# Three attention branches summed in 32-row blocks turned by VectorE, a band mask in sixteen 32x32 tiles, and a new order of instructions

## The chip, the cores and the metric

The kernel runs on one core of a Trainium2 chip. A core has TensorE (PE, matmuls into PSUM), VectorE (DVE), ScalarE (ACT) and GpSimd (POOL), and SyncE (SP), which issues the transfers. The metric is the device time of the whole program in microseconds: the median of three runs before the change was 1501.98 us (1499.52 to 1504.33).

## The reference

The input `x` has 8 batch rows of 512 tokens and 256 features. After a layer norm, three results are added to `x`: an attention with three branches, a gated feed-forward layer of 1024 features, and a mixture of 1024 rank-one experts of which 8 are chosen for each of 4 expert heads. All matrices are float32. The attention has 16 heads of 16 features, and its part that matters here is, per head and token:

```python
# compressed: 16 tokens of k and of v make one block (32 blocks)
logits_c = where(pos >= blk_end, q @ k_c.T / 4, NEG)
out_c = softmax(logits_c) @ v_c * any(pos >= blk_end)
# selected: the tokens of the 4 blocks with the highest logits_c
out_s = softmax(where(tok <= pos, q @ k_s.T / 4, NEG)) @ v_s
# local: the last 32 tokens
out_l = softmax(where(0 <= pos_q - pos_k <= 32, q @ k.T / 4, NEG)) @ v
gates = softmax(mean over heads of q @ Wg + bg)          # three per token
out = (gates[0] * out_c + gates[1] * out_s + gates[2] * out_l) @ Wo
```

No softmax is normalised before its product with `v`: each `v` carries a column of ones, so a product gives 16 sums and their denominator, 17 columns per head. The sums are divided, weighted with the gate and added at the end. This is the "branch sum" of the title.

## The kernel before, in words

The work is cut into 32 tiles of 128 tokens (four per batch row, `i` = 0 to 3) and 16 halves of 256 tokens for the feed-forward layer. For each tile, row or half there are generator functions, one for each stage, and each says which engine and which buffers its next piece needs. A `Conductor` (L209) runs all of them at build time: it books each instruction on its engine with a price (`price`, L233: so much per column and a fixed part, 0.36 us for an issue by SyncE) and takes next the stage that can start first, ties broken by a rank. `PLAN` (L116) shifts the ranks, tile by tile. What comes out is one fixed order of instructions per engine, with semaphores where they depend on each other. At run time an engine takes its queue strictly in that order, so an instruction that waits holds all that stands behind it. Every instruction is emitted by one helper, so the profile names L202 for all of them; I go by the tiles (`acs`, `at`, `wT` and so on).

Eight PSUM banks are shared by all: two pairs for the attention logits, four single banks for everything else. The stages around the change are:

- `gates` (L657): the three gates per token of a row, `gt`, tokens on partitions.
- `queries` (L767): `q` of a tile, and the compressed logits for all 32 blocks of the row, masked by a matmul with the identity that adds `cmask`.
- `select` (L855): picks the four blocks on VectorE; GpSimd subtracts each head's maximum from the compressed logits into `ec`.
- `compressed` (L955): ScalarE exponentiates `ec`, TensorE transposes it (`ecT`), and four matmuls with the block-diagonal `vc17` give the compressed sums, tokens on partitions. VectorE divides them by the 17th column and multiplies by the gate into `atc`.
- `weights` (L987): logits of the local and the selected branch, keys on partitions, 32-row tiles of TensorE, four at a time. The local ones get the band mask by four matmuls of 128x128 by 512 columns with the identity and `bandT`. ScalarE exponentiates into `wT`.
- `products` (L1046): `wT` times `v17`, with four heads in the four 32-row groups of the output: 17 of the 32 rows are sums. Two banks hold selected and local branch for all heads, tokens along the columns.
- `finish` (L1081) with `by_token` (L938): for each of the two banks ScalarE copies it to `acs`, TensorE transposes it (4 transposes) into another bank, so that tokens are on partitions; VectorE divides and weights the two branches into `at2`; GpSimd adds them and `atc`; TensorE transposes the sum (`at`), and ScalarE copies it to `attnT`, features on partitions.
- `project` (L1311): adds the expert part and `attnT` times `wo`, and stores the tile.
- `route` (L1194): four chains of GpSimd products (`big`) per tile, which build the weights of all 1024 experts from VectorE's `chosen`. `hidden` (L1269) with `fetch` (L1261): the feed-forward layer, whose weights `wb` are loaded again by SyncE for each half into two buffers.

Of the kernel before, what the change touches and what calls it, by code (L numbers as in the profile page):

```python
# [16 lines left out]
P = 128  # L17
# [25 lines left out]
    ("ident", P), ("any", 1), ("slot", 8), ("fold", 2 * P), ("head4", H), ("last", 2),  # L43
]
_BF_COLS = [
    ("identb", P), ("win", P + WIN), ("caus", P), ("causT", P), ("bandT", P), ("prevT", WIN),
# [17 lines left out]
def shape_constants():  # L64
# [21 lines left out]
    put("head4", p // NB == np.arange(H)[None] % 4)  # L86
# [6 lines left out]
    putb("bandT", np.where((q - p >= 0) & (q - p <= WIN), 0.0, OUT))  # L93
# [14 lines left out]
def bc(ap, axis, n):  # L108
# [8 lines left out]
    "-10",  # L117
    "-12",
    "-5 -5 2 -1 -3 -11 0 -1",
    "-30 5 0 -14 0 -5 12 -4",  # L120
    "0 7 6 -4 0 0 10 4",
    "-7 5 4 0 9 25 -10 6",
    "-1 3 -1 23 3 14 4 -30 -30 -2 -7 -11 -2 -20 4 3 -9 -6 30 1 3 -1 3 4 2 14 -7 2 6 -8 10 23",
    "-3 0 2 -4 8 0 0 -4 -2 0 -4 -1 -7 -4 1 0 3 2 0 -7 0 2 0 1 -21 -2 0 -3 23 -9 7 -10",
    "-1 0 24 30 12 4 10 0 29 4 -1 -30 5 3 1 0 20 26 6 30 0 9 1 13 18 -1 13 16 -10 16 28 21",
    "4 0 -5 0 0 3 3 -27 0 -5 -6 -30 -15 -28 2 -16 8 6 -13 9 -29 -25 0 -13 -17 12 3 -6 0 -14 28 "
    "2",
    "-1 7 7 0 11 -14 18 -30 0 -12 1 -12 -2 19 0 -7 8 0 0 0 7 0 6 -24 -24 -28 13 -19 10 -23 -21 "
    "7",
    "-19 -18 12 -8 0 -17 -3 -20 -19 3 1 0 -4 -14 -1 -12 -1 -26 9 2 7 5 -1 -2 3 -14 -9 -12 0 0 "  # L130
    "8 -11",
    "0 -4 -25 -23 4 -7 -17 -30 -30 -2 -1 -29 -13 -30 -2 -11 -24 0 -4 -27 -28 -30 9 -3 -9 -2 "
    "-27 0 0 -9 2 16",
    "0 -7 -21 -2 -1 -5 -7 -6 0 -30 0 -25 -3 -3 10 -3 7 0 17 15 6 12 0 0 0 2 22 5 29 -28 30 0",
    "-6 0 0 16 5 10 -8 5 17 -14 1 8 -26 -9 0 0 4 0 2 4 -10 -7 1 -3 14 -27 26 -3 15 2 -10 13",
    "-3 1 0 0 3 0 -3 -4 1 2 2 -30 0 -10 3 1 3 -5 0 -4 10 2 0 7 11 0 6 0 0 -2 14 28",
    "-14 9 -8 -1 -10 -3 1 27 -13 0 3 1 -7 1 -4 6 -12 -24 -2 1 3 -18 -6 7 21 1 -2 9 -13 0 4 15",
    "-2 -29 0 -7 3 -1 -30 0 0 -18 -3 0 11 0 11 -10 -12 0 -7 30 -27 -24 0 -3 -13 -1 16 8 1 -10 "
    "24 23",
    "-1 0 -10 0 0 -30 -7 18 -3 2 11 1 -11 11 -20 7 -7 4 0 7 8 -3 12 -5 0 4 -25 8 -25 0 -14 12",  # L140
    "20 1 0 -3 7 6 18 7 -18 4 -8 1 -14 -6 1 -8",
    "0 7 0 -7 0 -3 7 1 0 4 0 0 -2 -3 8 15",
    "-16 19 19 6 -10 6 -8 15 1 0 -5 1 7 6 12 21 -20 15 26 3 -4 -7 -1 -8 -9 -5 6 9 -9 -15 -25 0",
    "-28 10 -28 13 -3 0 4 -11 0 12 19 -21 -5 -14 28 -26 -2 0 26 17 13 -29 25 -23 17 0 0 26 -2 "
    "7 12 0",
# [60 lines left out]
class Conductor:  # L206
# [26 lines left out]
    def price(self, eng, op, args, kw):  # L233
# [3 lines left out]
        if eng == "PE":  # L237
            self.tiling = (P, P)
            if op == "transpose":
                cost = 0.109  # L240
            else:
                n = int(np.prod(args[2].shape[1:]))
                cost = n * 0.433e-3 if args[2].dtype == BF16 else max(n * 1.69e-3, 0.223)
                if self.share > 1:
                    k, m = args[1].shape[0], int(np.prod(args[1].shape[1:]))
                    self.tiling = tuple(32 if a <= 32 else 64 if a <= 64 else P for a in (k, m))
                    each = 1.05 if m > 32 else 0.97 if n > 64 else 1.25
                    cost = max(n * 0.423e-3 * each, 0.017)
        elif eng == "SP":
            cost = 0.36  # L250
        else:
# [4 lines left out]
            if eng == "POOL" and any(a.dtype == BF16 for a in aps):  # L256
                cost += 0.24e-3 * n
            if op in ("match_replace", "max_index", "tensor_tensor_reduce", "reciprocal"):
                cost += 0.08
# [69 lines left out]
def tile_kernel(ctx, tc, x, wq, wk, wqT, wv, wo, bdk, bdv, wga, bga, wgu, bg, bu, wd, bd,  # L329
# [64 lines left out]
    ident, identb = const("ident"), bconst("identb")  # L394
    cmask = bconst("cmask").rearrange("p (i n) -> p i n", n=NB)
# [37 lines left out]
    vc17s = stock("vc17_", 2, [P, H * D1])  # L433
    for st_, fill in ((v17s, 1.0), (vl17s, 0.0), (vc17s, 0.0)):
# [7 lines left out]
    for it in vc17s.items:  # L442
        pool.tensor_copy(by_head(it[0])[:, :, D], const("head4"))
# [23 lines left out]
    gts = stock("gt", 3, [P, 3, NT])  # L467
# [8 lines left out]
    ecTs, acss = stock("ecT", 1, [P, 4, P]), stock("acs", 2, [P, 4, P])  # L476
    rzs = stock("rzn", 3, [P, 16])
    atcs, at2s = stock("atc", 2, [P, 16, D]), stock("at2", 2, [P, 2, 2, 4 * D])
# [20 lines left out]
    for e in con.at:  # L499
        con.at[e] = 0.0  # L500

# [155 lines left out]
    def gates(s, pg):  # L657

        s.gt = yield DVE, gts
        gt, gm = s.gt.ap, buf_gm  # L660
# [13 lines left out]
        vec.tensor_tensor(gt[:, 2, 0:1], gt[:, 2, 0:1], const("any"), ALU.mult)  # L674
        s.done("gates")
# [3 lines left out]
    def prepare_values(s):  # L679
# [53 lines left out]
        s.vc17 = yield None, vc17s  # L733
        vc17 = s.vc17.ap
        pt = yield PE, banks
        pvt = pt.ap[:, :2 * P].rearrange("p (c n) -> p c n", c=2)
        for f in range(2):
# [4 lines left out]
        vec.tensor_tensor(by_head(vc17)[:, :, :D], pvt.rearrange("p c (h d) -> p (c h) d", d=D),  # L742
                          bc(const("head4"), 2, D), ALU.mult)
# [7 lines left out]
    def release_row(s):  # L751
# [8 lines left out]
        for it in (s.vc17, s.v17, s.vl17):  # L760
            it.free()
        yield None, s.tiles[-1].ev("at0"), s.tiles[-1].ev("at1")
        s.gt.free()
# [3 lines left out]
    def queries(t):  # L767

        s, i = t.row, t.i
        yield None, s.ev("xn"), came["wq_s"]  # L770
# [13 lines left out]
        pt, t.lg = yield PE, banks, lgs  # L784
        for a in range(2):
            mm(pt.ap[:, a * 8 * NB:(a + 1) * 8 * NB], t.q.ap[:, a, :],
               s.kcbd.ap[:, a].rearrange("p h n -> p (h n)"), start=a == 0, stop=False,
               skip_group_check=True)
        pc = pt.ap.rearrange("p (h n) -> p h n", n=NB)
        first = i * (P // G)  # L790
        mm(pc[:, :, first:], identb, bc(cmask[:, i, first:], 1, H), start=False, stop=True,
           skip_group_check=True)
        yield ACT,
        act.copy(t.lg.ap[:, :, 4:], pc)
# [60 lines left out]
    def select(t):  # L855
# [13 lines left out]
        pool.tensor_tensor(t.ec.ap, lg[:, :, 4:], bc(mx, 2, NB), ALU.subtract)  # L869
# [68 lines left out]
    def by_token(acs, dst, gates):  # L938

        pt = yield PE, banks  # L940
        p4 = pt.ap.rearrange("p (a g d) -> p a g d", a=4, g=4)
        for a in range(4):
            pe.transpose(p4[:, a].rearrange("p g d -> p (g d)"), acs.ap[:, a, :], ident)
        acs.free()
        rzn = yield DVE, rzs
        po = p4.rearrange("p a g d -> p (a g) d")
        vec.reciprocal(rzn.ap, po[:, :, D])
        for b in range(2):
            c = slice(8 * b, 8 * b + 8)
            vec.scalar_tensor_tensor(dst[:, c], po[:, c, :D], gates[:, b:b + 1],  # L950
                                     bc(rzn.ap[:, c], 2, D), ALU.mult, ALU.mult)
        pt.free()
        rzn.free()

    def compressed(t):  # L955

        s, i = t.row, t.i
        yield ACT, t.ev("ec")
        act.activation(t.ec.ap, t.ec.ap, AF.Exp)
        pt, ecT = yield PE, banks, ecTs  # L960
        for g in range(4):
            pe.transpose(heads4(pt.ap)[:, g, :],
                         t.ec.ap[:, 4 * g:4 * g + 4, :].rearrange("p h n -> p (h n)"), ident)
# [4 lines left out]
        yield None, s.ev("vc"), s.ev("gates")  # L968

        pt = yield PE, banks  # L970
        w = 4 * D1
        for g in range(4):
# [445 lines left out]
```

## Time and profile before

| what | value |
|---|---|
| median of three runs | 1501.98 us |
| the profiled execution | 1506.37 us in all, span of its instructions 1504.3 us |
| TensorE granted clock, mean | 0.989 |
| idle of TensorE, 0 to 35 us / 35 to 200 / 200 to 1470 / 1470 to 1505 | 16.5 / 11.7 / 32.2 / 3.9 us |
| longest waits of GpSimd | 164.6 us for VectorE's `chosen` |
| longest waits of ScalarE | for TensorE's PSUM: 160.4 (`xg`), 140.5 (`wT`), 123.8 us (`aT`) |
| DMA | 83.5 MB, mean 56 GB/s |

The page gives for each engine its busy time, its share of the span and its count of instructions. A group's line has the engine, the operation, what it writes and reads, the shape, the count, then the busy time in us, the mean of one in ns, and the engine's idle time just before them with what ended it. The timeline has start and length in us. TensorE's matmuls are pipelined, so their lengths overlap, and the distance between two starts tells more than a length. A float32 matmul leaves two records, a transpose and a bf16 matmul one.

### The profile page before, as it was taken

The numbers are of one execution on the slowest core, as the hardware profiler recorded it, in microseconds if no ns is written. First come the engines' busy times: TensorE is split into PE (matmuls) and PEld (weight loads), VectorE is DVE, ScalarE is ACT, GpSimd is POOL, SyncE is SP. The second block draws the span as 40 slices with busy tenths as digits, with TensorE's granted clock in tenths as the row PEclk, the third lists the DMA queues.
The fourth block names the chain that finished last, engine by engine and source line by source line (L and its number), as shares of the span: only waits on it lengthen the run. The fifth ranks groups of instructions, "written<-read, shape, count | busy, mean of one in ns | idle before, by whom it ended". The sixth has DMA issues, their size and how long they took to land.

```text
span 1504.3 us, 44379 instructions
## 1 busy us (share of the span) xinstructions
PE 1440.8 (96%) x17312; PEld 1126.9 (75%) x17312; DVE 1300.7 (86%) x5207; ACT 649.0 (43%) x1292; POOL 962.5 (64%) x948
## 2 busy tenths in 40 slices
PE   5899998999999999999999999999999999999999
PEld 4677777777777777777877778777877777877777
DVE  3989889979989988899889896989798978999992
ACT  3534451544354445452544425444434435344253
POOL 3546756755567566874675756777636775577676
PEclk9899999999999999999999999999999999999999
DMA  8111111212112112121122212022120112111120
GB/s 287 44 45 50 36 53 32 80 46 60 47 31 79 45 43 58 51 62 51 30 61 62 60 47 62 25 67 59 48 66 26 55 48 60 52 27 52 37 59 19
DMA packets 100018, 83.52 MB, mean 56 GB/s; under 512 B 23265, under 2 KB 80609, under 8 KB 99681
## 3 DMA queue, kind: packets, MB, share of 16 engines
q1 hardware_dynamic: 99808, 80.69, 18.4%
q8 instruction: 136, 2.23, 0.6%
q14 instruction: 74, 0.60, 0.1%
HBM read 49.67 MB, written 4.19 MB: 36 GB/s over the span
## 4 chain that ended last, share of the span: by engine, by line
PE 66%; DVE 24%; ACT 3%; issue 2%; POOL 2%; DMA 2%; SPq 0%; DVEq 0%; ACTq 0%; POOLq 0%
PE psum L202 66%; DVE bm L202 3%; DVE pick L202 2%; DVE big L202 1%; POOL big L202 1%; DVE sums L202 1%; DVE chosen L202 1%; DVE ml L202 1%; DVE at_x L202 1%; DVE aT L202 1%; ACT wT L202 1%; DVE hT L202 1%; DVE xg L202 1%; DVE mr L202 1%; DVE at L202 1%
## 5 line engine op out<-in xcount | busy, mean ns | idle before, releaser
L202 POOL TENSOR_TENSOR big<-chosen,ed 128x1024 f32<-128x1024 bf16 x128 | 275.1, 2149 | 250.1 <-DVE chosen L202 164.6
L202 ACT ACTIVATE wT<-psum 128x1024 f32<-128x1024 f32 (+1 forms) x224 | 218.4, 1024 | 149.6 <-PE psum L202 140.5
L202 PE MATMUL psum<-xnT,wb 128*128 128x256 f32 x1024 | 250.4, 388 | 9.2 <-DVE hT L202 6.9
L202 POOL TENSOR_TENSOR big<-big,ed 128x1024 f32<-128x1024 f32 x128 | 248.6, 1942 | 9.9
L202 PEld LDWEIGHTS psum<-xnT,wb 128*128 128x128 f32 x1024 | 187.4, 191 | 45.4 <-DVE hT L202 9.2
L202 DVE TENSOR_REDUCE bm<-psum 128x32 f32<-128x512 f32 (+2 forms) x224 | 199.5, 912 | 18.6 <-PE psum L202 18.2
L202 POOL TENSOR_TENSOR big<-big 128x512 f32<-128x512 f32 x128 | 141.0, 1102 | 9.6
L202 PE MATMUL psum<-wT,v 128*32 128x128 f32 (+1 forms) x3584 | 127.6, 278 | 7.4 <-ACT wT L202 5.3
L202 ACT ACTIVATE xg<-psum,bg_s 128x256 f32<-128x256 f32 x128 | 60.9, 476 | 162.0 <-PE psum L202 160.4
L202 PEld LDWEIGHTS psum<-xnT,deT_s 128*128 128x128 f32 x1024 | 122.1, 193 | 10.5 <-issue 4.9
L202 PE MATMUL psum<-xnT,deT_s 128*128 128x128 f32 x1024 | 127.0, 277 | 0.0
L202 PE MATMUL psum<-wd_s,hT 128*128 128x256 f32 x512 | 124.7, 387 | 1.2 <-DVE hT L202 0.8
L202 PE MATMUL psum<-ue_s,aT 128*128 128x256 f32 x512 | 121.8, 384 | 0.2 <-DVE aT L202 0.2
L202 PEld LDWEIGHTS psum<-wT,v 128*32 128x32 f32 (+1 forms) x3584 | 90.5, 110 | 40.3 <-ACT wT L202 16.5
L202 DVE SCALAR_TENSOR_TENSOR aT<-aT,psum 128x512 f32<-128x512 f32 x128 | 86.6, 680 | 27.3 <-ACT aT L202 23.5
L202 PEld LDWEIGHTS psum<-ue_s,aT 128*128 128x128 f32 x512 | 94.0, 190 | 21.3 <-issue 5.4
L202 PEld LDWEIGHTS psum<-wd_s,hT 128*128 128x128 f32 x512 | 94.0, 192 | 20.6 <-issue 4.2
L202 PE MATMUL psum<-k,q 32*128 32x384 f32 (+3 forms) x1024 | 98.0, 474 | 5.8 <-DMA k<-kT 5.7
L202 DVE TENSOR_TENSOR chosen<-rc 128x1024 bf16<-128x1024 bf16 x128 | 99.4, 776 | 0.0
L202 POOL TENSOR_TENSOR gw<-big 128x256 f32<-128x256 f32 x128 | 90.6, 707 | 10.0
L202 PE MATMUL psum<-qx,k 32*128 32x128 f32 (+1 forms) x2560 | 94.3, 282 | 1.8 <-ACT wT L202 1.3
L202 PEld LDWEIGHTS psum<-qx,k 32*128 32x128 f32 (+1 forms) x2560 | 78.4, 182 | 21.9 <-issue 14.6
(158 smaller groups left out, 2911.3 us busy)
## 6 DMA issues: line engine op xcount, KB each, us to landing
wb<-in_wgu SPq DMA_DIRECT2D x128, 256.0 KB, 2.7
qx<-qT SPq DMA_DIRECT2D x96, 64.0 KB, 1.9
qx<-xT SPq DMA_DIRECT2D x96, 64.0 KB, 1.9
yo<-in_x SPq DMA_DIRECT2D x32, 128.0 KB, 2.1
q<-qT SPq DMA_DIRECT2D x64, 64.0 KB, 2.0
k<-kT SPq DMA_DIRECT2D x16, 256.0 KB, 2.5
out<-yo SPq DMA_DIRECT2D x32, 128.0 KB, 1.7
kw<-k SPq DMA_DIRECT2D x48, 80.0 KB, 2.5
```

The lines of the kernel that those rows point to most:

```text
L202: return f(*a, **k)
```

## The change

Five things change together.

1. Compressed logits are computed and masked for the `nb` = 8 (i + 1) blocks that can be seen, not for all 32; `ec` is laid out with the four head groups inside.
2. The compressed product is turned round: `vcq` is the stationary operand and `ecT` moves, so its sums come out like those of `products`, 32 rows per head group, tokens along the columns. `products` writes the columns in four runs of 32 tokens.
3. `acs`, `by_token`, `at2`, `atc` and the last transpose go. VectorE turns the three banks out of PSUM by 32x32 blocks into `accT` (one buffer), so that tokens are on 32 partitions, by block and head. A new stage `join` divides (48 denominators per partition in one reciprocal), multiplies by the gates on VectorE, weights and adds on GpSimd, and turns the sum back by 32x32 blocks into `attnT`.
4. For that the gates are needed by token in a block and for each head group: SyncE copies them with 16 small transfers per row from `gt` to `gx`.
5. The band mask becomes 16 matmuls of 32x32 by 512 columns, each in its own tile of TensorE (four row groups by four column groups), with a table `bandR` in place of `bandT`.

The planner's prices get two additions (the sixteen tiles, GpSimd's memset), SyncE's queue is booked as busy until 21 us at the start, and `PLAN` has new numbers throughout, so the order of instructions differs on every engine. In the order that results, SyncE issues the spreads of the first `k` and `q` directly behind the constants, where two `wb` chunks and four `yo` loads stood first.

```diff
-        for a in range(2):
-            mm(pt.ap[:, a * 8 * NB:(a + 1) * 8 * NB], t.q.ap[:, a, :],
-               s.kcbd.ap[:, a].rearrange("p h n -> p (h n)"), start=a == 0, stop=False,
-               skip_group_check=True)
+        pc = pt.ap[:, :H * nb].rearrange("p (h n) -> p h n", n=nb)
+        for a in range(2):
+            mm(pc[:, 8 * a:8 * a + 8], t.q.ap[:, a, :], s.kcbd.ap[:, a, :, :nb], start=a == 0,
+               stop=False, skip_group_check=True)
...
-        mm(pc[:, :, first:], identb, bc(cmask[:, i, first:], 1, H), start=False, stop=True,
+        mm(pc[:, :, first:], identb, bc(cmask[:, i, first:nb], 1, H), start=False, stop=True,
...
+        s.gx = yield SP, gxs
+        for c in range(4):
+            for g in range(4):
+                sp.dma_start(out=s.gx.ap[32 * g:32 * g + 32, c], in_=gth.ap[32 * c:32 * c + 32])
...
-        for g in range(4):
-            mm(pt.ap[:, g * w:g * w + w], ecT.ap[:, g, :], s.vc17.ap[:, g * w:g * w + w],
-               start=g == 0, stop=g == 3, skip_group_check=True)
+        pc = pt.ap.rearrange("p (b j q) -> p b j q", b=4, j=4)
+        for j in range(4):
+            mm(pc[:, :, j, :], s.vcq.ap[:, j, :], ecT.ap[:, j, :].rearrange("p (b q) -> p b q", b=4),
+               start=j == 0, stop=j == 3, skip_group_check=True)
...
-        rzn = yield DVE, rzs
-        po = by_head(pt.ap[:, :H * D1])
-        vec.reciprocal(rzn.ap, po[:, :, D])
-        vec.scalar_tensor_tensor(t.atc.ap, po[:, :, :D], s.gt.ap[:, 2, i:i + 1], bc(rzn.ap, 2, D),
-                                 ALU.mult, ALU.mult)
+        t.accT = yield DVE, accTs
+        vec.transpose(t.accT.ap[:, 2].rearrange("p b j m -> p (b j m)"), pt.ap)
         pt.free()
...
+            if k is None:
+                con.share = 16
+                for c in range(4):
+                    for j in range(4):
+                        r = slice(32 * j, 32 * j + 32)
+                        mm(heads4(es[j // 2].ap[32 * c:32 * c + 32, j % 2]), identb[r, r],
+                           bc(bandR[r, c], 1, 4), start=False, stop=True, skip_group_check=True,
+                           tile_position=(32 * j, 32 * c))
+                con.share = 1
...
-            acs, at2h = yield ACT, acss, at2s
-            act.copy(acs.ap, heads4(t.acc[jp].ap))
-            t.acc[jp].free()
-            at2 = at2h.ap
-            yield from by_token(acs, at2.rearrange("p b j (g d) -> p (b j g) d", d=D),
-                                s.gt.ap[:, 0:2, i])
...
-            pt = yield PE, banks
-            pe.transpose(pt.ap[:, :P], at, ident)
-            at2h.free()
-            yield ACT,
-            act.copy(t.attnT.ap[:, jp, :], pt.ap[:, :P])
+            yield DVE, t.ev("pv"), t.ev("acc2")
+            vec.transpose(t.accT.ap[:, 0:2, :, 2 * jp:2 * jp + 2, :].rearrange("p r b j m -> p r b (j m)"),
+                          t.acc[jp].ap.rearrange("p (r b n) -> p r b n", r=2, b=4))
+            t.acc[jp].free()
...
+    def join(t):
+        s, i = t.row, t.i
+        yield None, s.ev("gates")
+        yield DVE, t.ev("acc0"), t.ev("acc1")
+        acc = t.accT.ap.rearrange("p r b j m -> p r (b j) m")
+        vec.reciprocal(rz3.rearrange("p r b j -> p r (b j)"), acc[:, :, :, D])
+        vec.tensor_tensor(rz3, rz3, bc(s.gx.ap[:, :, i, :].rearrange("p b r -> p r b"), 3, 4), ALU.mult)
+        t.done("rz")
+        yield POOL,
+        part = t.accT.ap.rearrange("p r b j m -> p (r b j) m")[:, :, :D]
+        pool.tensor_tensor(part, part, bc(rz3.rearrange("p r b j -> p (r b j)"), 2, D), ALU.mult)
+        pool.tensor_tensor(acc[:, 0, :, :D], acc[:, 0, :, :D], acc[:, 1, :, :D], ALU.add)
+        ath = yield POOL, ats
+        at = ath.ap
+        pool.tensor_tensor(at, acc[:, 0, :, :D], acc[:, 2, :, :D], ALU.add)
+        t.accT.free()
+        t.attnT = yield DVE, attnTs
+        vec.transpose(t.attnT.ap.rearrange("p a (b q) -> p b a q", b=4),
+                      at.rearrange("p (b a j) d -> p b a (j d)", b=4, a=2))
+        ath.free()
+        t.done("attn")
```

## The prediction

> **What bounds the kernel now.** I read the engines' shares and the chain on the page, then a table of stages, then TensorE's timeline, then the groups by shape.
>
> ```profile
> PE 1440.8 (96%) x17312; PEld 1126.9 (75%) x17312; DVE 1300.7 (86%) x5207; ACT 649.0 (43%) x1292; POOL 962.5 (64%) x948
> ...
> PE 66%; DVE 24%; ACT 3%; issue 2%; POOL 2%; DMA 2%; SPq 0%; DVEq 0%; ACTq 0%; POOLq 0%
> ```
>
> By stage (us, then busy us of TensorE, its weight loads, VectorE, ScalarE and GpSimd, the granted clock, DMA share and GB/s):
>
> ```profile
> 0.00:35.00 35.00, 18.53 (x146) 13.46 (x146) 12.38 (x59) 11.54 (x24) 12.34 (x24) 0.94 0.89 302
> ...
> 200.00:1470.00 1270.00, 1237.82 (x14912) 971.64 (x14916) 1134.63 (x4524) 554.38 (x1100) 833.33 (x812) 1.00 0.18 51
> 1470.00:1505.00 35.00, 31.14 (x419) 24.33 (x418) 9.72 (x19) 11.08 (x16) 22.67 (x20) 1.00 0.03 9
> ```
>
> TensorE is the bound: from 200 to 1470 us it is busy 1238 of 1270 us, so only 32 us are left there for better ordering, and time must come out of TensorE's own work. VectorE is second at 89% of that stage, and the chain passes through it for 24% of the span. ScalarE (44%) and GpSimd (66%) have room. The clock was 1.00 after 200 us, so prices taken there are full-speed prices.
>
> TensorE overlaps its instructions, so I price a group from its start to the next group's start:
>
> ```profile
> 706.52 0.45 PE L202 MATMUL psum<-qx,kw 32*32 32x32 f32 x32
> 706.90 0.23 PE L202 MATMUL psum<-cbf 128*128 128x128 bf16 x1
> ...
> 710.58 1.04 PE L202 MATMUL psum<-cbf 128*128 128x512 bf16 x4
> 711.46 1.00 PE L202 MATMUL psum<-vc,ecT 128*128 128x68 f32 x8
> 712.30 0.43 PE L202 MATMUL psum<-wv_s,xnT 128*128 128x259 f32 x1
> ...
> 730.59 0.60 PE L202 MATMUL psum<-cst,acs 128*128 128x128 f32 x4
> 731.03 0.38 PE L202 MATMUL psum<-cst,vtok 128*128 128x128 f32 x2
> ```
>
> Four transposes take 731.03 - 730.59 = 0.44 us, 0.11 each. The band mask takes 711.46 - 710.58 = 0.88, 0.22 per 512 columns. Thirty-two records of 32x32 tiles take 0.38, 0.012 each. Eight records of only 68 columns take 0.84, about 0.105 each, as much as 128 columns would: the weight load of 128 f32 columns sets the floor (an f32 matmul leaves two records).
>
> **TensorE, part by part.** *Transposes*: eight of `acs` and two of `at` per tile go, 320 x 0.11 = -35.2 us. *Band mask*: 32 x 0.88 = 28.2 go. Sixteen tiles of 512 columns come: the nearest rows give 16 x 0.012 to issue plus 0.22 for the last to stream, 0.41 per tile, 13.1 in all; net -15.1. No row shows more than four tiles at once. If four is all, sixteen passes cost 4 x 0.22 = 0.88 and nothing is saved; if they issue as fast as single records can follow each other here (0.007), 0.33 and 17.6 are saved. I take the middle value, since its 32x32 row is the nearest. The Trainium skill (TensorE: Matmul & The Clock Gate, Measured speedup vs the span model) gives 10.6x for exactly this packing; by that, an estimate of 16 x 0.22 / 10.6 = 0.33 us, 2.6 us less in all; no run here shows it yet. *Changes of tile shape*: the instruction orders hold 658 of them before and 678 after; a 128-column pass started 0.20 us before its successor where the shape changed and 0.11 where not, so 20 x 0.09 = +1.8. *Compressed logits*: four records per tile of 256 columns (0.216 each) shrink to 64, 128, 192 and 256 for i = 0 to 3. By the floor just read, 0.112, 0.112, 0.162, 0.216: 4 x (0.104 + 0.104 + 0.054) = 1.05 per batch row, x 8 = -8.4. Their bf16 mask goes from 512, 384, 256, 128 columns to 128 each: (0.16 + 0.107 + 0.053) x 8 = -2.6. The compressed product has four f32 matmuls before and after, 68 against 128 columns: 0 by the same floor. That the products now write their 128 columns in four runs of 32 costs nothing: the logits' mask of 384 columns in sixteen runs of 24 took 0.163, the rate of an unbroken one. TensorE's sum: -35.2 - 15.1 + 1.8 - 8.4 - 2.6 = **-59.5 us**.
>
> **Start.** TensorE stood 5.74 us before 34.58 for `k` from SyncE's queue, where two weight chunks and four `yo` loads went first. In the new order the `k` and `q` spreads stand directly behind the constants, some 6 us earlier: **-5.7**, late next being TensorE's own queue. The bf16 constants grow from 544 to 640 KB; GpSimd, which waits for them, was done with them at 14.2 us, so that is hidden.
>
> **VectorE.**
>
> ```profile
> L202 DVE SCALAR_TENSOR_TENSOR aT<-aT,psum 128x512 f32<-128x512 f32 x128 | 86.6, 680 | 27.3 <-ACT aT L202 23.5 <-PE psum L202 2.1 <-ACT wT L202 1.0
> ...
> L202 DVE SCALAR_TENSOR_TENSOR at<-psum,gt,rzn 128x128 f32<-128x128 f32 x128 | 39.0, 347 | 2.6
> ...
> L202 DVE TENSOR_TENSOR yo<-psum,yo 128x256 f32<-128x256 f32 x64 | 26.8, 418 | 28.6 <-PE psum L202 28.1
> ...
> L202 DVE RECIPROCAL rzn<-psum 128x16 f32<-128x16 f32 x96 | 24.0, 250 | 17.0 <-PE psum L202 16.6
> ...
> L202 DVE SCALAR_TENSOR_TENSOR atc<-psum,gt,rzn 128x256 f32<-128x256 f32 x32 | 15.5, 484 | 1.4
> ```
>
> Out: 39.0 + 24.0 + 15.5 = 78.5 us. In, per tile: three 128x512 block transposes out of PSUM, one 128x256 in SBUF, a reciprocal and a product of 48 columns. No row shows a block transpose. From below I take the 512-column row at 0.68 and the 256-column row at 0.42 (one column per step); from above twice these. I choose the lower, because every f32 form out of PSUM here runs at that rate. Sum 3 x 0.68 + 0.42 + 0.25 + 0.30 = 3.0, x 32 = 96.3: **+18 us of VectorE**, covered only while TensorE is the longer queue. At the upper end it is +97.
>
> The rule that speaks against this change is the Trainium skill's (TensorEngine Tiling, PSUM Bottleneck): tiling does not speed the emptying of PSUM, so share that between ScalarE and VectorE. Here 64 ScalarE copies of 0.60 us on the 44% engine become transposes on the 89% one; the rule gives no number.
>
> **GpSimd and ScalarE.**
>
> ```profile
> L202 POOL TENSOR_TENSOR big<-big,ed 128x1024 f32<-128x1024 f32 x128 | 248.6, 1942 | 9.9
> ...
> L202 POOL TENSOR_TENSOR big<-big 128x512 f32<-128x512 f32 x128 | 141.0, 1102 | 9.6
> ...
> L202 POOL TENSOR_TENSOR gw<-big 128x256 f32<-128x256 f32 x128 | 90.6, 707 | 10.0
> ...
> L202 POOL TENSOR_TENSOR at<-at 128x128 f32<-128x128 f32 x64 | 33.9, 529 | 74.2 <-DVE at L202 73.1 <-PE psum L202 1.2
> L202 POOL TENSOR_TENSOR at<-at,atc 128x128 f32<-128x128 f32 x64 | 32.3, 504 | 5.0
> ```
>
> Out 66.2. In: 768 columns (1.52, between the first two rows) and two of 256 (0.71): 2.94 per tile, 94; the narrower `ec` gives back 9: +22, to 68%. ScalarE loses 64 copies (35.5 + 17.0 us) and gains nothing. Neither sets the end.
>
> **SyncE.** Sixteen gate copies per row are issued by SyncE. Its nearest row, the 32-partition `vl` copies:
>
> ```profile
> L202 SPq DMA_DIRECT2D vl<-v x96: 591/620/1797, 36.0 to 1289.2; - x96
> ```
>
> 16 x 0.65 (0.62 and the gap to the next) = 10.4 us in one block, where the planner books 0.36 each, 5.8. Behind them stand hidden-layer weights, `q` and `kw`, which TensorE waits for in order. Nothing late: 0; all 4.6 us late in each of 8 rows: 37. The two weight buffers (3.5 us of TensorE work) and other work between cover most of it; I take 8.
>
> **New waits at VectorE.** In the long stage its share goes from 1135/1270 = 89% to about 1150/1217 = 94.5%. TensorE then meets a late VectorE more often. From 0 to 40 us (TensorE's idle of today, 32 us, somewhat more than doubled); I take 7.
>
> **Sum.** 1504.3 - 59.5 - 5.7 + 8 + 7 = 1454 us of span. The profiled execution took 1506.4 in all, 2.1 more than its span, and the median of the runs is 1502.0, 4.4 below it: 1454 + 2.1 - 4.4 = 1452, say **1450 us**.
>
> **Rivals.** (1) *VectorE becomes the bound*: a transpose takes two steps per column. VectorE's 1301 + 97 = 1398 and the 22.6 + 25.3 = 48 us in which it stands idle in the first and the last stage make 1446; with 2.5% of waits (TensorE's own 32 of 1270 today), 1482. For: 24% of the chain. Against: the rate of all neighbouring rows. (2) *The sixteen tiles do not overlap*: 15 us of gain are lost, 1465. (3) *Nothing new is waited for*: 1435, and the order may save 5 to 10 more of the 32 us of idle. (4) *Slower*: there is a single `accT`, so VectorE's transpose of the next tile's compressed sums stands in VectorE's queue until GpSimd has done three operations (2.94 us) on this tile, and those may stand behind one expert chain (2.15 + 1.94 + 1.10 + 0.71 = 5.9 us). All behind VectorE's queue waits too. VectorE has 1504 - 1319 - 48 = 137 us of room, so it decides from 137 / 32 = 4.3 us per tile; at 60% of 8.8, 5.3 us, VectorE needs 1319 + 48 + 169 = 1536. Against: GpSimd waited 165 us for `chosen` alone, so it is seldom behind. (5) *It does not move*: waits eat 50 us, 1500.
>
> **Numbers.** Forecast (1435 to 1465) 0.58; rival 1 0.14; rival 2 beyond 1465 0.07; rival 3 below 1435 0.08; rival 5 0.03; rival 4 0.10. The range runs from 1428 (rival 3 with a better order) to 1482 (sixteen tiles in a row and half of the new waits' upper bounds, or most of rival 1); what lies outside is rivals 4 and 5 and the end of rival 1. Within 0.3%, about what a measurement of this kernel can tell from no change, is 1497.5 to 1506.5. Faster 0.86, same 0.03, slower 0.11.
>
> **What would show it.** `acs` and `at` gone from TensorE; the sixteen mask tiles starting some 0.2 us apart in all and ending within 0.45; block transposes at 0.68 and 0.42; VectorE near 1319 busy; the first `k,q` near 29. Wrong if TensorE's idle in the long stage exceeds 60 us, or if VectorE's idle is put down to GpSimd's `accT` or `at`, or TensorE's to `wb`.

## The result, and the profile after

The changed kernel takes 1512.63 us (median of 7 runs, 1509.21 to 1516.19), the kernel before 1501.98 in the same comparison. The ratio is 1.0063, 95% interval 1.0044 to 1.0083: **slower by 0.6%**, about 9.5 us. The forecast was 1450.

The page of the changed kernel, first busy time, then the chain that ended last (it breaks off early in this trace, so its shares say little):

```profile
PE 1404.3 (93%) x17376; PEld 1094.1 (72%) x17376; DVE 1326.6 (88%) x5143; ACT 591.1 (39%) x1164; POOL 989.8 (66%) x924
...
DVE 4%; PE 2%; POOL 1%; ACT 0%; issue 0%; ACTq 0%; POOLq 0%; DVEq 0%
```

TensorE lost 36 us of busy time, and yet the span grew from 1504.3 to 1510.5 us. The table of stages of the changed kernel (columns as before):

```profile
0.00:35.00 35.00, 20.98 (x170) 14.66 (x170) 13.88 (x65) 13.47 (x27) 10.11 (x21) 0.96 0.88 299
35.00:200.00 165.00, 149.22 (x1777) 117.47 (x1774) 146.20 (x586) 66.41 (x144) 93.69 (x90) 0.95 0.19 52
200.00:1470.00 1270.00, 1205.72 (x14974) 940.78 (x14972) 1153.17 (x4473) 499.81 (x979) 859.81 (x790) 0.99 0.17 50
1470.00:1505.00 35.00, 26.61 (x455) 20.30 (x456) 12.47 (x19) 11.46 (x15) 25.56 (x25) 0.80 0.06 17
```

In the long stage TensorE now stands idle for 1270 - 1206 = 64 us, where it was 32; and the clock fell, to 0.80 in the last stage. So I split every span into four: the gaps between TensorE's records ("idle"), half of the time at which the granted clock is 0.5 ("clock loss", with up to 1 us of a half-clock stretch that runs on past the last instruction), 3 us behind its last record, and the rest ("work at full speed").

| kernel | median us | ratio to before, 95% interval | work | idle | clock loss |
|---|---|---|---|---|---|
| before | 1501.98 | 1 | 1423.0 | 60.4 | 17.7 |
| **after** | 1512.63 | 1.0063 [1.0044, 1.0083] | 1367.3 | 103.0 | 37.0 |
| e1_no_gx | 1489.59 | 0.9901 [0.9878, 0.9925] | 1368.3 | 90.7 | 24.5 |
| e2_short_turn | 1496.56 | 0.9954 [0.9936, 0.9972] | 1362.9 | 94.4 | 35.5 |
| e8_both | 1475.57 | 0.9806 [0.9784, 0.9829] | 1364.2 | 78.1 | 32.2 |
| e7_gates_pe | 1496.58 | 0.9945 [0.9925, 0.9964] | 1370.2 | 90.4 | 31.0 |
| e3_mask4 | 1512.19 | 1.0051 [1.0030, 1.0072] | 1378.5 | 95.3 | 37.8 |
| e4_before_mask16 | 1496.81 | 0.9956 [0.9941, 0.9971] | 1412.8 | 61.7 | 17.7 |
| e12_before_two_parts | 1494.19 | 0.9944 [0.9931, 0.9958] | 1401.7 | 68.0 | 21.9 |
| e6_before_noplan | 1641.21 | 1.0903 [1.0880, 1.0926] | 1448.4 | 139.9 | 47.9 |
| e5_after_noplan | 1609.61 | 1.0704 [1.0682, 1.0726] | 1374.8 | 153.4 | 76.4 |
| e10_before_reorder | 1500.00 | 0.9975 [0.9961, 0.9989] | 1418.1 | 65.2 | 15.0 |
| e9_after_reorder | 1495.48 | 0.9947 [0.9924, 0.9970] | 1366.2 | 93.2 | 33.8 |
| e11_gates_reorder | 1493.69 | 0.9929 [0.9908, 0.9949] | 1374.8 | 89.4 | 20.5 |
| e13_before_light | 1489.21 | 0.9903 [0.9886, 0.9921] | 1416.8 | 52.7 | 15.0 |
| e14_two_parts_light | 1478.26 | 0.9827 [0.9806, 0.9849] | 1395.4 | 56.4 | 21.2 |
| e15_both_light | 1453.61 | 0.9671 [0.9652, 0.9689] | 1356.7 | 69.2 | 22.1 |
| e16_after_light | 1491.05 | 0.9919 [0.9901, 0.9937] | 1355.4 | 90.8 | 39.8 |

The last three columns are those of the one profiled execution of each kernel, which lay up to 4.5 us from its median. The clock loss wanders most: by the mean granted clock it was 35 to 42 us in the executions of after, and 8 to 21 us (median 12) in those of before.

The first two rows are the riddle: 55.7 us of work went, 42.6 us of idle and 19.3 us of clock loss came. Below, a difference between two kernels is that of their ratios times 1503 us. What TensorE waited for in the changed kernel (us in total, times, longest):

```profile
PE psum L204 <- DVE hT L204: 20.0, 14, 3.4
PE psum L204 <- ACT wT L204: 14.0, 22, 2.2
...
PE psum L204 <- DVE aT L204: 10.8, 11, 2.9
PE psum L204 <- DMA wb<-in_wgu: 10.5, 3, 4.7
PE psum L204 <- DMA qx<-xT: 6.9, 4, 3.8
PE psum L204 <- DVE accT L204: 6.3, 5, 2.7
```

and in the kernel before:

```profile
PE psum L202 <- DVE hT L202: 8.3, 10, 3.4
PE psum L202 <- ACT wT L202: 6.6, 13, 1.6
PE psum L202 <- DMA k<-kT: 5.7, 1, 5.7
...
PE psum L202 <- DVE aT L202: 2.6, 5, 1.1
```

Two kinds are new: waits for transfers (`wb`, `qx`: 17.4 us where there were none), and longer waits for VectorE and ScalarE in places that waited before (`hT`, `wT`, `aT`: 44.8 against 17.5 us).

By place, much of it sits in the end. These are the last 60 us of TensorE's work, in the kernel before and in the changed one (columns as in the table of stages):

```profile
1441.10:1501.10 60.00, 59.34 (x856) 46.99 (x854) 34.28 (x124) 30.01 (x50) 43.95 (x43) 1.00 0.13 37
```

```profile
1447.30:1507.30 60.00, 45.96 (x658) 33.91 (x658) 32.59 (x111) 18.06 (x24) 37.95 (x36) 0.80 0.04 11
```

Before, TensorE stood idle for 0.7 of these 60 us, at full clock. In the changed kernel it is 14.0 us of idle and, at 0.80, 12 us of clock loss: 25 of the 62 us that came are here. What is missing there is the feed-forward layer. Its last matmuls (`wd_s`) stand 5 us before TensorE's end in the kernel before, and 109 us before it in the changed one, where TensorE then waits for one short chain after another:

```profile
1494.99 1.03 PE L202 MATMUL psum<-wd_s,hT 128*128 128x256 f32 x4
```

```profile
1394.68 3.62 PE L204 MATMUL psum<-wd_s,hT 128*128 128x256 f32 x16
...
1476.44 0.33 PE L204 MATMUL psum<-qx,kw 32*32 32x32 f32 x8 [2.47 <-DMA qx<-xT]
...
1479.10 0.69 PE L204 MATMUL psum<-cst,ext 128*128 128x128 f32 x2 [1.24 <-POOL ext L204]
...
1483.63 1.08 PE L204 MATMUL psum<-wT,v 128*32 128x128 f32 x16 [1.23 <-ACT wT L204]
```

### The profile page after: what moved, and what is told of

The parts are those of the page before. It is cut to its first block, busy times and chain, and to the rows that moved or that the text cites. A ratio compares the mean times of both kernels' runs of the same rounds, so it can differ in the third digit from the quotient of the medians.

```text
span 1510.5 us, 44434 instructions
## 1 busy us (share of the span) xinstructions
PE 1404.3 (93%) x17376; PEld 1094.1 (72%) x17376; DVE 1326.6 (88%) x5143; ACT 591.1 (39%) x1164; POOL 989.8 (66%) x924
## 5 line engine op out<-in xcount | busy, mean ns | idle before, releaser
L204 PE MATMUL psum<-xnT,wb 128*128 128x256 f32 x1024 | 257.9, 396 | 28.8 <-DVE hT L204 14.7
L204 PEld LDWEIGHTS psum<-xnT,wb 128*128 128x128 f32 x1024 | 191.8, 196 | 64.7 <-DVE hT L204 19.0
L204 PE MATMUL psum<-ue_s,aT 128*128 128x256 f32 x512 | 127.2, 387 | 1.5 <-DVE aT L204 1.1
L204 PEld LDWEIGHTS psum<-ue_s,aT 128*128 128x128 f32 x512 | 93.2, 191 | 21.1 <-issue 5.9
L204 PE MATMUL psum<-qx,k 32*128 32x128 f32 (+1 forms) x2560 | 99.5, 288 | 1.1 <-ACT big L204 0.6
L204 PEld LDWEIGHTS psum<-qx,k 32*128 32x128 f32 (+1 forms) x2560 | 83.2, 187 | 21.2 <-issue 12.1
L204 DVE TENSOR_TENSOR chosen<-rc 128x1024 bf16<-128x1024 bf16 x128 | 96.2, 752 | 0.0
```

The costliest lines, as they stand in the source:

```text
L204: return f(*a, **k)
```

## The experiments

Theory A: the block of sixteen gate copies in SyncE's queue holds back `wb`, `q` and `qx`. Theory B: VectorE's new load makes it late. Theory C: the order of instructions, planned with wrong prices, is at fault. Theory D came later: work taken from TensorE counts little because VectorE is the next to be late.

### SyncE's sixteen copies (e1, e7)

SyncE's queue in the changed kernel, then TensorE's (start, length, and in brackets its idle time):

```profile
72.80 10.72 SPq L204 DMA_DIRECT2D gx<-gt  x16
83.62 0.52 SPq L204 DMA_DIRECT2D wb<-in_wgu  x1
```

```profile
80.81 1.08 PE L204 MATMUL psum<-wT,v 128*32 128x128 f32 x32
86.55 3.46 PE L204 MATMUL psum<-xnT,wb 128*128 128x256 f32 x8 [4.66 <-DMA wb<-in_wgu]
```

The weight chunk goes out 0.10 us behind the block, and TensorE stands for 4.66 us until it lands. The same picture stands at 574.65 us (4.37 us, behind a block of 11.39). e1 takes the copies out and leaves the order:

```diff
-                sp.dma_start(out=s.gx.ap[32 * g:32 * g + 32, c], in_=gth.ap[32 * c:32 * c + 32])
+                con.book("SP", "dma_start", (), {...})   # booked, not issued; gx is a constant
```

> The changed kernel without SyncE's 128 small gate copies; gx holds a constant instead, so the gates are left out of the result. The planner still books them, so every other instruction stands where it stood. Theory A (SyncE's block of 16 copies, 10 to 11.7 us in the profile where the planner books 5.8, delays wb, q and qx): TensorE's waits for DMA (20 us in the changed kernel's profile) go, and with them some of the half-clock windows: 1475 to 1492 us. Theory B (VectorE's load and lateness eat the gain): less than 8 us, 1504 to 1513. Theory C (both only follow from an order that was planned with wrong prices): something between, 1490 to 1505.

Measured 24 us less than after. The waits for `wb` are gone from the list, `qx` fell to 2.8, and the clock loss fell by 12.5 us with them. Theory A holds, and the clock is about half of its price (12 of 24 us in the profiled executions, about 10 by the mean granted clock of all). e7 keeps the gates and spreads them by TensorE:

```diff
+        nc.vector.tensor_tensor(gs, bc(gth.ap, 1, 4), bc(bc(const("head4"), 2, NT), 3, 3), ALU.mult)
...
+            for f in range(2):
+                nc.tensor.matmul(pt.ap[:, 2 * P:2 * P + 48], const("fold")[:, f * P:(f + 1) * P],
+                                 s.gs.rearrange("p c i n -> p (c i n)"), start=False, stop=f == 1,
+                                 skip_group_check=True)
+            nc.scalar.copy(s.gx.ap.rearrange("p c i n -> p (c i n)"), pt.ap[:, 2 * P:2 * P + 48])
```

> The changed kernel, with the gates spread by TensorE in place of SyncE's 128 transfers: per batch row one VectorE product of 48 columns, two float32 matmuls of 48 columns with the constant `fold` into unused columns of a bank that is in use anyway, and one ScalarE copy of 48 columns into `gx`. The planner still books the 128 transfers, so that all other instructions keep their order; the computation is complete. Theory A (SyncE's block of sixteen issues holds back wb, q and qx): the gain of leaving the copies out altogether is kept but for 16 records x 0.1 us and 8 x 0.15 us on the other engines, so 1491 us, ratio 0.991, and TensorE's waits for DMA fall from 20 to some 6 us. Rival (the copies cost little and the time went because a whole dependency was absent, the gates of the row coming late to the reciprocal's product): about as the changed kernel, 1505 to 1512.

It gains 18 us on after, not 21, and it is a complete kernel that beats both. DMA waits are down to 2.8 us; 4.7 us came back as TensorE's wait for `gs`, since the two matmuls stand in its queue too early.

### VectorE's transposes (e2, e8)

VectorE's and GpSimd's groups of the changed kernel that answer to those of before:

```profile
L204 DVE SCALAR_TENSOR_TENSOR aT<-aT,psum 128x512 f32<-128x512 f32 x128 | 86.0, 677 | 15.3 <-ACT aT L204 9.0 <-PE psum L204 5.9
...
L204 DVE STREAM_TRANSPOSE accT<-psum 128x512 f32<-128x512 f32 x96 | 64.9, 697 | 33.8 <-PE psum L204 22.4 <-POOL at L204 11.2
...
L204 DVE TENSOR_TENSOR rz<-rz,gx 128x48 f32<-128x48 f32 x32 | 17.0, 530 | 1.1
...
L204 DVE RECIPROCAL rz<-accT 128x48 f32<-128x48 f32 x32 | 14.2, 445 | 0.2
L204 DVE STREAM_TRANSPOSE attnT<-at 128x256 f32<-128x256 f32 x32 | 13.8, 430 | 5.6 <-POOL at L204 5.6
```

```profile
L204 POOL TENSOR_TENSOR accT<-accT,rz 128x768 f32<-128x768 f32 x32 | 50.0, 1562 | 54.6 <-DVE rz L204 53.4 <-DVE t L204 0.5
L204 POOL TENSOR_TENSOR accT<-accT 128x256 f32<-128x256 f32 x32 | 25.8, 805 | 2.5
L204 POOL TENSOR_TENSOR at<-accT 128x256 f32<-128x256 f32 x32 | 24.5, 764 | 2.2
```

The block transposes cost one column a step, as forecast (0.68 and 0.42); the reciprocal 0.445 instead of 0.25, and the product 0.53 instead of 0.30. e2 cuts the three transposes out of PSUM to 32 columns and books them in full:

```diff
-        vec.transpose(t.accT.ap[:, 2].rearrange("p b j m -> p (b j m)"), pt.ap)
+        con.book("DVE", "transpose", (t.accT.ap[:, 2].rearrange("p b j m -> p (b j m)"), pt.ap), {})
+        nc.vector.transpose(t.accT.ap[:, 2, 0, 0, :], pt.ap[:, :32])
```

> The changed kernel with the three block transposes out of PSUM cut to 32 of their 512 columns (the rest of the branch sums is left out, accT holds a constant there); booked in full, so the order and all waits stay. VectorE loses about 3 x 0.5 us per tile, 48 us. Theory A: VectorE is not what holds TensorE, under 10 us gained, 1503 to 1513. Theory B: most of it shows, 1465 to 1485. Theory C: 1485 to 1503.

16 us less than after, for 48 us less of VectorE. e8 joins e1 and e2:

> The changed kernel without the 128 gate copies (gx a constant) and with the three block transposes out of PSUM cut to 32 of 512 columns; all are booked as before, so the order of instructions stays. Left out: the gates and most of the branch sums. Theories A and B as two separate causes: the two gains measured alone add up, 1512.6 - 23 - 16 = 1473 us, ratio 0.980, and half-clock time falls to about 47 us. Rival, one cause (VectorE's lateness, with the DMA waits only a place where it shows): 1486 to 1490. If only these two made the new waits, TensorE's idle should come near that of before, 60 us; the runs alone left 91 and 94, so I expect about 80, and what stays above 60 belongs to the order.

39 us less than after, where 24 and 16 add up to 40: two separate causes. But with both gone the kernel has 59 us less TensorE work than before and is only 29 us faster. Idle is still 18 us and clock loss 14 us above those of before. Of these 32 us, 23 lie in its last 60 us of TensorE's work, so neither the copies nor the transposes make the end:

```profile
1414.40:1474.40 60.00, 46.89 (x668) 34.24 (x666) 30.80 (x111) 18.28 (x25) 39.04 (x36) 0.83 0.05 14
```

### TensorE's work alone (e3, e4, e12)

If a microsecond of TensorE's work counted as one of the span, these three would show it. e3 puts the band mask of after back to four matmuls, e4 puts the sixteen tiles into the kernel before; the order stays in both.

> The changed kernel with the band mask as four matmuls of 128x128 again, booked as the sixteen, so the order stays. If TensorE's work is still what counts, 32 x (0.88 - 0.41) = 15 us come back: 1525 to 1530. If the waits have taken over and swallow TensorE's work, 0 to 6 us: 1512 to 1519.

> The kernel before with the band mask alone as sixteen 32x32 tiles, booked as the four, so the order is that of before. By the prediction's step 15 us less, 1487; if its order has no room either (waits come due instead), 0 to 6 us less, 1496 to 1502; if the sixteen did not overlap, 1502.

e3: 11 us more work, no change of the time that shows (1.0051 against 1.0063, with intervals that overlap; the medians differ by 0.4 us). e4: 10.2 us less work, 6.6 us gained. e12 adds the narrow compressed logits to e4, so VectorE and SyncE get nothing new:

```diff
-            mm(pt.ap[:, a * 8 * NB:(a + 1) * 8 * NB], t.q.ap[:, a, :],
-               s.kcbd.ap[:, a].rearrange("p h n -> p (h n)"), start=a == 0, stop=False,
+            nc.tensor.matmul(pc[:, 8 * a:8 * a + 8], t.q.ap[:, a, :], s.kcbd.ap[:, a, :, :nb],
+                             start=a == 0, stop=False, skip_group_check=True)
```

> The kernel before with the two parts of the change that only take work off TensorE: the band mask as sixteen tiles (run alone: 1496.8 us, 6.6 us of the 15 priced) and the compressed logits computed, copied, subtracted and exponentiated for the visible blocks alone (priced at 8.4 + 2.6 us of TensorE). Both are booked as before, so all instructions keep their order, and VectorE and SyncE get nothing new; the computation is complete. If TensorE's work counts one to one, 1503 - 26 = 1477 us. If it counts as it did for the mask (6.6 of 15), 1503 - 0.44 x 26 = 1491 to 1492 us, with TensorE's idle up by what does not count. Theories A and B together say that nothing is lost to new waits here, since neither SyncE nor VectorE got work, so idle should stay within 8 us of 60 and half-clock time within 10 us of 36.

21.3 us less work, 8.4 us gained: idle +7.6, clock loss +4.2. The one-to-one number, 1477, is missed by 17 us without any new load elsewhere; 5 of the 17 are work that was priced at 26 us and came to 21. The idle (68.0) only just stayed within the 8 us that theories A and B allow.

### The order (e5, e6, e9, e10, e11)

e5 and e6 empty `PLAN` in both kernels (`PLAN = [""] * 24` and `* 23`).

> The changed kernel with all shifts of rank set to nothing (every stage in the order of its plain rank), so without the searched order. Theories A and B (the new waits belong to the edit, whatever the order): the difference from the kernel before without its shifts is small, as it is with them, within 15 us either way. Theory C (the order searched with wrong prices is at fault, the edit itself is good): it is faster than the kernel before without its shifts by 35 us or more, of the 56 us of TensorE's work that went. The times themselves are not known; with plain ranks I expect 30 to 120 us more than with the searched order, 1540 to 1630.

> The kernel before with all shifts of rank set to nothing: the base for the run before it. 1540 to 1640 us. Theories A and B: within 15 us of the changed kernel without its shifts. Theory C: at least 35 us slower than that.

Here the change **gains** 30 us, twice what A and B allow and just short of the 35 that C asked for; of 73.6 us less work, 41% arrives. So the searched order of before was worth 136 us to it and that of after only 96 to the other. This pair holds the whole change, copies and transposes included, so it does not weigh TensorE's work alone. And in these two orders the last `wd_s` matmuls stand 6 us (e5) and 7 us (e6) before TensorE's end, and the last 60 us hold 10.0 and 10.9 us of idle and clock loss: the costly end comes with the searched order of after, not with the change alone.

e10, e9 and e11 differ from before, after and e7 in `PLAN` (e11 also in the place of its two matmuls).

> The kernel before with another PLAN and nothing else: a new search that starts from its own PLAN and ranks each order by replaying it engine by engine, each engine strictly in its order, with the durations of the profiled run, 0.66 us for each issue by SyncE, and TensorE at half speed for 3.4 us after any 3.4 us in which it stood idle for more than 45%. It is the base for the next two runs, which got the same search for the same time. Little is left to save here, TensorE idle is 60 us and half speed costs 18: I expect 5 to 20 us of gain, 1483 to 1498 us. Theory C (the changed kernel's own order is the fault): the next run then gains at least 15 us more than this one. Theories A and B (the edit brings the waits with it in any order): both gain alike.

> The changed kernel with another PLAN and nothing else, found by the same search for the same time, from its own PLAN. Theory C: the order that knows SyncE's true issue time moves the sixteen gate copies to where nothing is late behind them, and its gain is 25 us or more, 1487 us or less (what leaving the copies out brought), below the kernel before with its new order. Theories A and B: the copies and the transposes cost what they cost wherever they stand, the gain is that of the kernel before, 5 to 20 us, 1492 to 1508 us, and it stays above the other.

> The changed kernel with the gates spread by TensorE, as two runs ago (1496.6 us), and another PLAN from the same search; the two matmuls are also put a little later, so that TensorE does not stand before them (it waited 4.7 us there). The computation is complete. Gain of the search 5 to 20 us as in the other two, and 4 us from the two matmuls: 1473 to 1488 us, ratio about 0.985. If half-clock windows follow TensorE's waits, half-clock time falls with its idle, from 62 us; if they come from elsewhere, it stays near 62.

The 45% in the search's replay is a setting, not a measurement. Before gained 4 us, after 17, which is 14 more: just short of the 15 that C asked for, with its other number (1487 or less) missed, and no equal gain either. The mechanism that C named is refuted: the waits for transfers stayed (20.4 us, now 18.5); 9 us of the gain are in the waits for VectorE (48.9 to 39.9 us). With its new order the changed kernel stands at 0.9947 against 0.9975; the intervals overlap, so which of the two is faster stays open. e11 missed its range by 6 us and has the lowest ratio of the complete kernels here that keep the change, with an interval that overlaps those of e7, e9 and e12. In its profiled execution the clock loss is 10 us below that of e7 while the idle stayed, but most of that is chance: the mean clock there was 0.987, in its other executions 0.981 to 0.985, in those of e7 0.979 to 0.984. Both new orders of the changed kernel keep its end: the last 60 us hold 23.6 us (e9) and 21.2 us (e11) of idle and clock loss.

### A lighter VectorE (e13 to e16)

These four take the block maxima of the logits over 2 of each 16 and leave the other 14 out, to make VectorE lighter while the order stays:

```diff
-                    vec.tensor_reduce(bm[:, 0], sp_[:, :, 0].rearrange("p j (n e) -> p j n e", e=G),
-                                      AX.X, ALU.max)
+                    se = sp_[:, :, 0].rearrange("p j (n e) -> p j n e", e=G)
+                    con.book("DVE", "tensor_reduce", (bm[:, 0], se), {})
+                    nc.vector.tensor_reduce(bm[:, 0], se[:, :, :, :2], AX.X, ALU.max)
```

> The base for the next three runs: the kernel before with VectorE lightened. The block maxima of the logits (`bm`, 224 reductions, 198 us in the page of after) are taken over 2 of each 16 logits, booked in full, so the order stays and VectorE has some 160 us less to do, 1140 instead of 1300. Left out: 14 of 16 logits in those maxima. The order was planned for the full times, so TensorE can only lose its waits for VectorE (23.5 us of idle) and some half speed: 1470 to 1490 us.

> The same lightening in the kernel with the two parts that take only TensorE work away (21 us of work there, which gained 8.4). Left out: 14 of 16 logits in the block maxima. Theory D (work taken from TensorE counts little because VectorE, at 87 to 94%, is then the next to be late): with VectorE at 76% it counts nearly one to one, 17 us or more below the lightened kernel before. Rival (it counts little because the order and its many short chains through ScalarE, DMA and GpSimd hold it, or because the clock answers): again 8 to 11 us.

> The lightening in the changed kernel without the gate copies and with short block transposes (59 us less TensorE work than before, which gained 27). Left out: 14 of 16 logits in the block maxima, the gates and most of the branch sums. Theory D: 45 to 59 us below the lightened kernel before. Rival: 25 to 32 us below it.

> The lightening in the changed kernel itself. Left out: 14 of 16 logits in the block maxima. Theories A and D: the 56 us of TensorE's work count nearly in full, SyncE's block still costs its 23 us, VectorE's transposes nothing: 28 to 35 us below the lightened kernel before. Rival, waits that belong to the order: about as far above or below it as without lightening, +10 us, or at best 10 us below it.

VectorE fell by 129 to 141 us. Against e13: e14 gains 11 us (rival's number), e15 35 (between the two numbers), e16 loses 2 (rival's number). Theory D falls as the main cause. VectorE's load explains a part: after against before shrinks from +9.5 to +2.4 us, but a microsecond of TensorE's work still counts 0.53 (e14: 11.4 of 21.4) and 0.58 (e15: 34.9 of 60.1), against 0.39 (e12) and 0.50 (e8) under the full VectorE.

The two lose theirs in different places. e15 has 16.5 us more idle and 7.1 us more clock loss than e13, and 22 of these 24 us lie in its last 60 us of TensorE's work, where e13 has 0.5 us of idle; ahead of that its saved work came nearly in full:

```profile
1388.00:1448.00 60.00, 47.73 (x755) 34.97 (x748) 28.83 (x114) 19.93 (x27) 39.33 (x36) 0.83 0.06 18
```

e14, whose end is that of the kernel before, lost its 10 us along the way. TensorE's waits in e15, with VectorE at 1154 us:

```profile
PE psum L204 <- DVE hT L204: 18.4, 14, 2.8
PE psum L204 <- ACT wT L204: 13.9, 20, 2.2
...
PE psum L204 <- DVE aT L204: 6.2, 4, 2.9
```

The waits for `hT` and `wT` are those of after, though VectorE has 173 us less to do. So they do not hang on VectorE's total. One of them in the changed kernel, which hangs on the place of the instructions, VectorE's queue and then TensorE's:

```profile
246.08 2.35 DVE L204 TENSOR_TENSOR sums<-top 128x256 f32<-128x256 f32 x1
...
251.58 0.41 DVE L204 SCALAR_TENSOR_TENSOR xg<-psum,xg 128x256 f32<-128x256 f32 x1
252.03 0.48 DVE L204 SCALAR_TENSOR_TENSOR hT<-psum,bu_s,xg 128x256 f32<-128x256 f32 x1
...
252.57 1.78 PE L204 MATMUL psum<-wd_s,hT 128*128 128x256 f32 x7 [3.09 <-DVE hT L204]
```

ScalarE had finished `xg` and its partner at 246.6, but VectorE's queue has seventeen instructions of the expert choice first, and the two that make `hT` start only at 251.6. TensorE has `wd` next in its own queue and nothing to put before it. In the order of before, the longest such wait was as long; there were ten instead of fourteen.

## Why the prediction was wrong, step by step

- **TensorE's work, -59.5**: right, -55.7 in the split of the span. Of the band mask, forecast -15.1, the split shows 10 (e4) to 11 us (e3), although its sixteen matmuls took 0.37 per tile (forecast 0.41), from their start to that of the next group; no run shows where the rest went:

```profile
715.80 0.43 PE L204 MATMUL psum<-cbf 32*32 32x512 bf16 x16
716.17 0.44 PE L204 MATMUL psum<-cst,vtok 128*128 128x128 f32 x2
```

- **Start, -5.7**: half right. The wait of the first spreads fell from 5.7 to 3.0 us (now for `q` at 33.0, not 29), so 2.7 came.
- **VectorE +18, GpSimd +22 busy**: busy time rose by 25.9 and 27.3. The transposes were right. The reciprocal of 48 columns was priced with a row of 16 columns, which is 6 us of it, and that row, 0.25 us, already spoke against "every f32 form out of PSUM here runs at that rate". The product took 0.53 for 0.30, another 7 us. GpSimd's +22 is also a slip: 94 - 66.2 - 9 gives 19.
- **SyncE's block, +8**: mis-sized. The bounds were 0 and 37, e1 shows 24: about half idle, half clock loss. That the clock would answer was not in the prediction.
- **New waits at VectorE, +7**: mis-sized; e2 shows 16 for the transposes out of PSUM.
- **The end of the order**: no term at all. The last 60 us hold 25 us of idle and clock loss more than before, and they hold them in e1 (24.6 in all), e2 (24.3) and e8 (23.3) too.
- **The sum** is the step that failed. It took TensorE's 59.5 us one to one off the span, because TensorE was busy for 97% of the long stage, and set 15 us of new waits against them. In place of the 15 came 62, 42.6 of idle and 19.3 of clock loss. With what the runs show, 55.7 - 24 - 16 - 25 = -9: slower by 9, measured 9.5. That is reckoned afterwards, two prices come from runs and one from the place in the traces, and so close a fit is partly luck. A busy share of 97% told that there was little idle time, not that none would come.
- **One to one**: in the four comparisons that change little but TensorE's work, a microsecond came through at about 0 (e3), 0.39 (e12), 0.53 (e14) and 0.65 (e4), each on 10 to 21 us of work and with some 2 to 4 us of uncertainty. That is no fixed factor: in e8 (0.50) and e15 (0.58) most of the loss is the end.
- **Rivals**: (5), waits of 50 us and no move, had a chance of 0.03 and was nearest, with 42.6 us of idle and 19.3 of clock loss. (4) did not decide: VectorE waited for GpSimd's `at` before `accT` once, 11.2 us in the last stage. (1) and (2) did not happen.
- **The signs of failure** named in advance all came true: idle of the long stage 64 us (limit 60), waits of TensorE for `wb`, and idle of VectorE put down to GpSimd's `at` (11.2 us and 5.6 us).

Not settled: what the end would cost in a better order. The plain ranks (e5) show that the change does not force it, but no run put feed-forward matmuls back into the end of the searched order, so that the 25 us would then go is argued, not shown. Open too is why e12 and e14, with the order and the end of the kernel before, kept only about half of what they saved. e14 rules out VectorE's total as the main cause, and the waits for `hT` and `wT` stay at their places (e15).

## What to carry to other kernels

When an engine's queue is full by the view of shares, its work is worth its price only if something else stands ready in the queue; taken out of an order that was made around it (e4, e12, e14), 0.4 to 0.65 of it came here. Look at the end of an order by itself, and see what work is left there to stand between the waits: here the feed-forward layer had run out, and 25 us went. Price what a change puts into the queue of a helper engine as a block: sixteen small issues of 0.6 us were 11 us in which nothing else went out. And take parts one by one: the mask and the narrow logits alone (e12, 0.9944) were faster than the whole change.

## What the hardware showed that I had not expected

- **A wait of two to five microseconds can halve TensorE's clock for the next 3.4 us.** Around the wait at 86.55 (columns as in the table of stages):

```profile
85.00:86.50 1.50, 0.00 (x0) 0.00 (x0) 0.00 (x0) 0.00 (x0) 0.00 (x0) 1.00 0.79 255
86.50:90.00 3.50, 3.45 (x12) 2.33 (x16) 0.00 (x0) 0.00 (x0) 0.00 (x0) 0.55 0.44 130
90.00:93.40 3.40, 3.40 (x60) 2.52 (x60) 2.53 (x6) 1.34 (x4) 0.32 (x1) 0.96 0.28 77
```

  Full speed during the wait, 0.55 right behind it, 0.96 after that. Waits of 2.41 us (at 649.4), 3.45 (175.7) and 4.37 (574.7) were followed by the same 3.4 us at 0.5, one of 3.09 us (252.6) was not. The whole costs 37 us in the profiled execution of after, 18 in that of before. The Trainium skill (TensorE: Matmul & The Clock Gate, HAM oscillation — how this bites in real kernels) puts the rule as no idle gaps above some 3.4 us; the wait of 2.41 us shows a shorter gap doing it here. The same page (What's actually happening) calls the window of 3.4 us free-running; that one wait of 3.09 us did not do it fits a window whose phase decides, which no run here tests.
- **VectorE's short products of two SBUF operands can take several times their length.** The changed kernel's `rz<-rz,gx` took 207 ns at least, 209 in the median and 2139 at most, and `sums<-top` 410, 746 and 2371. In the one shown above, GpSimd was in an operation of 2.32 us from 245.84 on, and the product ended 0.27 us behind it. The 96 transposes out of PSUM do not show it: they lie between 665 and 718 ns, though 55 of them began while GpSimd was in an operation.
- **A small copy inside SBUF holds SyncE's queue for 0.6 us**, however little it carries: 0.59 in the median for the 1.5 KB of a gate copy, where a `wb` chunk of 256 KB took 0.33.

```profile
L204 SPq DMA_DIRECT2D gx<-gt x128: 507/589/1897, 72.8 to 1257.9; - x128
...
gx<-gt SPq DMA_DIRECT2D x128, 1.5 KB, 1.7
```
